# Norm chain of layer 2 ahead of the sort's comparisons, and the sort's first turn one step later

## The chip, the cores and the metric

The kernel runs on one core of one Trainium2 chip, all in float32. The metric is the device time of one execution in microseconds (us); less is better. A core has five engines that work side by side, each through its own queue in order: TensorE (PE, matrix products), VectorE (DVE), ScalarE (ACT), GpSimd (POOL) and SyncE (SP, which here only issues DMA transfers; ACT and POOL issue some too).

## The reference, cut to what matters

The input is one image x of 1024 channels by 64 x 64 pixels. Four layers follow, each of the form `x = x + layer(groupnorm(x))` with 32 groups of 32 channels.

```python
x = x + L0(_gn(x))     # a scan over the channels
x = x + L1(_gn(x))     # einsum('oi,nihw->nohw', weight, x) + bias
x = x + L2(_gn(x))     # state-space layer: projections, convolution, tokens in a permuted order, scan, gate, projection
x = x + L3(_gn(x))     # einsum('oi,nihw->nohw', weight, x) + bias

def _mobius_perm(mobius, H, W):          # in L2: depends on the parameter `mobius` alone
    ...
        perms.append(jnp.argsort(score)) # one permutation of the 4096 tokens for each of two heads
```

Two things matter here. The group norm of layer 2 needs the mean and variance of layer 1's result over all pixels, so it can only be finished when layer 1 is. And the sort (`argsort`) depends on no activation, so its work can be done at any time ahead of layer 2's gather of tokens.

## The kernel before, in words

**Layer 1.** `pointwise` computes the 1024 x 1024 product by `run` and `multiply`: one level of a Strassen-like scheme, seven block products in place of eight. The image is cut into four pairs of 512-pixel columns (order 3, 2, 0, 1), and each pair's outputs into NG = 2 groups. So there are 4 x 2 x 7 = 56 steps, i = 0 to 55. In one step PE does one block product (8 matmuls of 128 x 128 by 128 x 512; the trace records each as two). The seven products of a group come in the order b21, b11, b22, t2, t3, t1, t4, named after the right-hand operand. After a product, DVE takes it out of PSUM: `put` (L963, one scalar_tensor_tensor with the bias) or `add` (L967, one tensor_tensor, and then L152, the batch norm statistics of the finished piece). Two products of a group accumulate on earlier ones: t2 and t1 go into the PSUM banks of b11, and t4 into those of t3. So a matmul that goes on in a bank comes after DVE's reading of it.

**What lies beside the products.** After each product, the body of the loop at L993 runs once. DVE, PE, POOL and ACT are under a manual schedule there: their queues hold the instructions in the order in which the Python code issues them. The body does, in this order:

- `next(sums, None)` (L994): sums of weights for later layers, on POOL (L454 to L457, L468, L481, L492), with their loads and stores on ACT's DMA queue. It yields True (`busy`) in a step in which it put work on POOL.
- `sort_on(not busy, n)` (L995): goes on with the sort. In a step that isn't busy it may issue up to n comparisons, n from a table by i % 14.
- the norm chain of layer 2 for the first four of the eight channel tiles (L996 to L1007), in steps 49 to 54 only.

**The sort** (`sort_work`, a generator) is a bitonic sort of 2 x 4096 keys that lie as 64 lines of 128. A comparison (`compare`, L351 to L360) is eleven small DVE instructions. From its eighth stage on (k > 7) the lines have to be turned: `turn_over` issues two transposes on PE (L370) into a PSUM tile, and a step later ("take") a copy on ACT (L372) into SBUF. Ahead of each turn stands one tensor_scalar on DVE (L399), which the transposes wait for. `sort_on` does at most one turn or take in a step. In layer 1 the first turn is issued in step 26, after product t1, and its copy in step 27.

**The norm chain** (`moments`, `norm_steps`, `rsqrt`), for tiles FIRST, is spread over steps:

| step | product | what is issued |
|---|---|---|
| 49 | b21 | four bn_aggr on DVE (L185, tile gn2a_mv) |
| 50 | b11 | matmul gn2a_pg on PE (L202): means over groups |
| 51 | b22 | three small DVE operations (L205 to L207, gn2a_d) |
| 52 | t2 | matmul gn2a_pv on PE (L211) |
| 53 | t3 | one DVE operation (L219, gn2a_v), then Ln and Exp on ACT (L172, L173) |
| 54 | t1 | four small DVE operations (L175 to L177, L222); two bn_aggr for the other tiles; four ACT operations (L948) that write the first operands of layer 2 |

In steps 49, 51 and 53 the body also issues two, three and two comparisons of the sort, and ahead of the chain's instructions. Steps 50 and 52 are busy for POOL and have none. The transposes of a later turn are issued in step 54.

**Queues around it.** PE's queue after step 50 is: product b11, gn2a_pg, product b22. ACT's queue around step 53 is: Ln, Exp, then the four stores of the last sum of weights (L500, tile s, 448 KB each), and then the first operands of layer 2. SP's queue has the weight loads (L827, into a ring of five buffers) and, behind them, the loads of layer 2 that need the space of these sums (L1232, L479).

```python
            busy = next(sums, None) if i % 14 < 13 else None
            sort_on(not busy, (0, 0, 0, 0, 3, 2, 1, 2, 1, 3, 3, 3, 0, 0)[i % 14])
            if i == last - 6:
                chain = norm_steps("gn2a", *moments("gn2a", FIRST), len(FIRST), finer=True)
            elif last - 6 < i < last - 1:
                next(chain)
```

Of the kernel before, what the change touches and what calls it, by code (L numbers as in the profile page):

```python
# [94 lines left out]
def tile_net(ctx: ExitStack, tc: tile.TileContext, x, par_d, cst_d, w_d, w2_d, dbcw_d, out):  # L95
# [5 lines left out]
    def ps_tp(name):  # L101
        return psum.tile([P, FB], F32, tag="tp", name=name)
# [57 lines left out]
    def finish_of(steps):  # L160

        while True:
            try:
                next(steps)
            except StopIteration as stop:
                return stop.value
# [13 lines left out]
    def moments(name, tiles, some=None, mv=None):  # L180

        if mv is None:
            mv = small.tile([P, 2, CT], F32, tag="gn_mv", name=f"{name}_mv")
        for i in range(len(tiles)) if some is None else some:
            nc.vector.bn_aggr(mv[:, :, i], stats[:, tiles[i]].rearrange("p a b -> p (a b)"))  # L185
        n = len(tiles)
        return mv if some is not None else (mv[:, 0, :n], mv[:, 1, :n])

    def columns(tiles, norm, norms):

        for i, ct in enumerate(tiles):
            norms[ct] = tuple(v[:, i : i + 1] for v in norm)
# [135 lines left out]
    def sort_work():  # L328

        eng, bits = nc.vector, 7
        flip = cst[: HEADS * NT, CST["flip"]]

        def compare(t, new, bit):
            def two(x):
                v = x.rearrange("p (u s l) -> p u s l", s=2, l=2 ** bit)
                return v[:, :, 0], v[:, :, 1]

            rows, _, w = t.shape
            a, b = two(t.rearrange("p c w -> p (c w)"))
            (ka, kb), (ia, ib) = two(t[:, 0]), two(t[:, 1])
            (ka2, kb2), (ia2, ib2) = two(new[:, 0]), two(new[:, 1])
            over = swap[0][:rows, :, : w // 2]
            same = swap[1][:rows, 0, : w // 2]
            step = swap[1][:rows, 1, : w // 2]
            def like(x):
                return x.rearrange("p (u l) -> p u l", l=2 ** bit)
            for i, (x, y) in enumerate(((ka, kb), (ia, ib))):  # L350
                eng.tensor_tensor(like(over[:, i]), x, y, ALU.is_gt)  # L351
            eng.tensor_tensor(like(same), ka, kb, ALU.is_equal)
            eng.tensor_tensor(same, same, over[:, 1], ALU.mult)
            eng.tensor_tensor(ka2, ka, kb, ALU.min)
            eng.tensor_tensor(same, same, over[:, 0], ALU.add)
            eng.tensor_tensor(like(step), ib, ia, ALU.subtract)
            eng.tensor_tensor(kb2, ka, kb, ALU.max)
            eng.tensor_tensor(step, step, same, ALU.mult)
            eng.tensor_tensor(ia2, ia, like(step), ALU.add)
            eng.tensor_tensor(ib2, ib, like(step), ALU.subtract)  # L360

        def negate(v):
            eng.tensor_scalar(v, v, -1.0, None, ALU.mult)

        def turn_over(t, new):
            rows, _, w = t.shape
            yield "turn"
            pt = ps_tp("sort")
            for c in range(2):
                nc.tensor.transpose(pt[:w, c * rows : (c + 1) * rows], t[:, c], ident[:rows, :rows])  # L370
            yield "take"
            nc.scalar.copy(new.rearrange("p c w -> p (c w)"), pt[:w, : 2 * rows])  # L372

        now, other = lines
        negate(now.rearrange("p c (u s l) -> p (c u) s l", s=2, l=2)[:, :, 1])
        for k in range(1, 13):
            if k > bits:
                t, t2 = turned_
                yield from turn_over(now, t)
                for bit in reversed(range(k - bits)):  # L380
                    yield "compare"
                    compare(t, t2, bit)
                    t, t2 = t2, t
                yield from turn_over(t, now)
            for bit in reversed(range(min(k, bits))):
                yield "compare"
                compare(now, other, bit)
                now, other = other, now
            if k + 1 < bits:
                v = now.rearrange("p c (u t s l) -> p (c u) t s l", t=2, s=2, l=2 ** k)  # L390
                negate(v[:, :, 0, 1])
                negate(v[:, :, 1, 0])
            elif k + 1 == bits:
                v = now.rearrange("p c (s l) -> p c s l", s=2)
                for s in range(2):
                    eng.tensor_scalar(v[:, :, s], v[:, :, s], flip[:, s : s + 1], None, ALU.mult)
            elif k < 12:
                i = k - bits + 2
                eng.tensor_scalar(now, now, flip[:, i : i + 1], None, ALU.mult)  # L399
        eng.tensor_copy(order_i, now[:, 1])  # L400
        yield "take"
        nc.gpsimd.dma_start(perm_d.rearrange("(a p) o -> a (p o)", p=P), order_i)
        yield "take"
        for h in range(HEADS):
            r0, full = h * LC + S, (NK - 1) * LT
            perm = perm_d[h * N : (h + 1) * N]
            for idx in (src, dst_):
                nc.gpsimd.dma_start(idx[r0 : r0 + LT, : NK - 1],
                                  perm[:full].rearrange("(k r) o -> r (k o)", r=LT))
                nc.gpsimd.dma_start(idx[r0 : r0 + N - full, NK - 1 :], perm[full:])  # L410
# [3 lines left out]
    def sort_on(quiet, n):  # L414


        while coming[0] is not None:
            was = coming[0]
            if was == "compare":
                if n == 0 or not quiet:  # L420
                    return
                n -= 1
            coming[0] = next(order, None)
            if was != "compare" or coming[0] != "compare":
                return
# [360 lines left out]
    def b_tile(name, k, pair):  # L786
        return bpool.tile([P, FB], F32, tag=name, name=f"{name}_{pair}_{k}")
# [157 lines left out]
    def normed(norm):  # L945
        def make(t, ct, nb):
            scale, bias = norm[ct]
            nc.scalar.activation(t, X[nb][:, ct, :], AF.Identity, bias=bias, scale=scale)  # L948
        return make


    def pointwise(name, m, bias_name, order, src, dst):
        norm = {}
        columns(range(CT), finish_of(norm_steps(f"gn{name}", mean1, var1)), norm)

        def before(pair):
            for nb in (2 * pair, 2 * pair + 1):
                if X[nb] is None:
                    load(nb, src)

        def put(m, o, nb, ps):
            part = X[nb][:, o, :]
            nc.vector.scalar_tensor_tensor(part, ps, pcol(bias_name, o), part, ALU.add, ALU.add)  # L963

        def add(m, o, nb, ps):
            part = X[nb][:, o, :]
            nc.vector.tensor_tensor(part, ps, part, ALU.add)  # L967
            take_stats(nb, o)

        def after(pair):  # L970
            for nb in (2 * pair, 2 * pair + 1):
                save(nb, dst)

        yield from run(order, [m], normed(norm), put, add, before, after, quick=True)
# [17 lines left out]
    with tc.manual_schedule(engines={E_.DVE, E_.PE, E_.Pool, E_.Activation}):  # L992
        for i, _ in enumerate(pointwise("l1", W1, "b1", [3, 2] + EARLY, x0_d, x1_d)):  # L993
            busy = next(sums, None) if i % 14 < 13 else None  # L994
            sort_on(not busy, (0, 0, 0, 0, 3, 2, 1, 2, 1, 3, 3, 3, 0, 0)[i % 14])  # L995
            if i == last - 6:  # L996
                chain = norm_steps("gn2a", *moments("gn2a", FIRST), len(FIRST), finer=True)
            elif last - 6 < i < last - 1:
                next(chain)
            elif i == last - 1:  # L1000
                columns(FIRST, finish_of(chain), norm2)
                mv2 = moments("gn2b", SECOND, range(2))
                name = f"{WX}_{EARLY[0]}"
                begun = {"name": name, **{b: [b_tile(b, k, name) for k in range(2)] for b in ("b21", "b11")}}
                for b, row in (("b21", 1), ("b11", 0)):
                    for k in range(2):
                        normed(norm2)(begun[b][k], row * KH + k, 2 * EARLY[0])  # L1007
        for _ in sums:
            pass
    sum_pool.__exit__(None, None, None)  # L1010
# [34 lines left out]
    with tc.tile_pool(name="l2a", bufs=2) as pa, tc.tile_pool(name="l2a2", bufs=1) as pa2, \  # L1045
# [185 lines left out]
        with tc.manual_schedule(engines={E_.DVE, E_.PE, E_.Pool, E_.Activation}):  # L1231
# [3 lines left out]
            ends, i, chain, quiet = iter(()), -1, None, False  # L1235
# [618 lines left out]
```

## Time and profile before

| what | value |
|---|---|
| time, median of 3 runs | 2684.88 us (2682.02 to 2690.34) |
| the profiled execution: time | 2685.99 us |
| the profiled execution: span of its records | 2684.1 us |
| PE busy | 2564.7 us (96% of the span) |
| DVE busy | 1833.2 us (68%) |
| POOL busy | 1215.3 us (45%) |
| ACT busy | 1079.5 us (40%) |
| mean granted TensorE clock | 0.984 of full speed |
| layer 1's products on PE | from 225 us to 626.7 us |

The span is the time from the first to the last record; some 1.9 us of the execution lie around it. The rest of the document uses these views. The list of waits says which instruction stood at the head of an engine's queue for how long, and whose end released it ("PE a <- DVE b"). A timeline gives start, duration, engine, line, operation, operands and count; in square brackets stands the idle time of the engine just ahead. The table by windows gives for each stretch the busy time of PE, PE's weight loads, DVE, ACT and POOL, with counts, and then the granted TensorE clock (1.00 is full speed), the DMA share and GB/s. A busy time includes time in which an instruction has started and is held inside its engine.

### The profile page before, as it was taken

The numbers are of one execution on the slowest core, as the hardware profiler recorded it, in microseconds if no ns is written. First come the engines' busy times: TensorE is split into PE (matmuls) and PEld (weight loads), VectorE is DVE, ScalarE is ACT, GpSimd is POOL, SyncE is SP. The second block draws the span as 40 slices with busy tenths as digits, with TensorE's granted clock in tenths as the row PEclk, the third lists the DMA queues.
The fourth block names the chain that finished last, engine by engine and source line by source line (L and its number), as shares of the span: only waits on it lengthen the run. The fifth ranks groups of instructions, "written<-read, shape, count | busy, mean of one in ns | idle before, by whom it ended". The sixth has DMA issues, their size and how long they took to land.

```text
span 2684.1 us, 30608 instructions
## 1 busy us (share of the span) xinstructions
PE 2564.7 (96%) x9520; PEld 1712.4 (64%) x9520; DVE 1833.2 (68%) x3870; ACT 1079.5 (40%) x1835; POOL 1215.3 (45%) x1100
## 2 busy tenths in 40 slices
PE   4788999999999999999999999999999999899998
PEld 3674444444555555444454448888888888788887
DVE  7996866655555564367787775677585775877877
ACT  3783110103556564466767663332233223312120
POOL 4154123242132243146474635566575565554544
PEclk9897999999999999999999999999999999999999
DMA  7245467547565577487667946889899798888896
GB/s 291 99 169 204 138 239 251 174 150 241 142 175 142 139 194 179 123 267 238 206 208 237 311 152 199 235 254 293 227 304 259 245 309 220 270 293 297 301 315 213
DMA packets 422741, 597.22 MB, mean 223 GB/s; under 512 B 141972, under 2 KB 210707, under 8 KB 419508
## 3 DMA queue, kind: packets, MB, share of 16 engines
q1 hardware_dynamic: 298020, 367.89, 43.4%
q10 hardware_dynamic: 91456, 136.33, 14.5%
q0 software_dynamic: 33104, 91.04, 13.3%
q8 instruction: 77, 1.26, 0.2%
q14 instruction: 84, 0.69, 0.1%
HBM read 435.10 MB, written 160.05 MB: 222 GB/s over the span
## 4 chain that ended last, share of the span: by engine, by line
PE 80%; DVE 10%; ACT 6%; DMA 2%; issue 1%; POOL 0%; DVEq 0%; ACTq 0%; SPq 0%; POOLq 0%
PE mm L844 36%; PE q_P5P L1728 5%; PE q_P6P L1728 5%; PE q_P7P L1728 5%; PE q_P3P L1728 5%; PE q_P4P L1728 5%; PE q_P2P L1728 5%; PE q_P1P L1728 5%; PE py L1375 2%; PE l2pt L1090 2%; DVE xt L632 1%; DVE cvp L1071 1%; DVE stats L554 1%; ACT b L948 1%; ACT xt L598 1%
## 5 line engine op out<-in xcount | busy, mean ns | idle before, releaser
L844 PE MATMUL mm<-t,w 128*128 128x512 f32 x1536 | 683.9, 596 | 0.0
L844 PE MATMUL mm<-b,w 128*128 128x512 f32 x1152 | 514.4, 598 | 4.0 <-ACT b L948 2.9
L844 PEld LDWEIGHTS mm<-t,w 128*128 128x128 f32 x1536 | 286.9, 191 | 323.1 <-issue 316.3
L844 PEld LDWEIGHTS mm<-b,w 128*128 128x128 f32 x1152 | 216.0, 191 | 252.3 <-issue 241.3
L1384 POOL DMA_INDIRECT y_rows<-g,dst x74 | 73.3, 990 | 184.3 <-ACT g L1380 171.7
L1071 DVE SCALAR_TENSOR_TENSOR cvp<-xs,par,cvp 128x512 f32<-128x512 f32 x128 | 95.3, 753 | 76.8 <-ACT cvp L1068 74.5
L1697 ACT COPY qQ<-q_P5P 128x512 f32<-128x512 f32 x48 | 28.1, 585 | 295.1 <-PE q_P5P L1728 288.8
L468 POOL TENSOR_TENSOR s<-s 128x256 f32<-128x256 f32 (+3 forms) x120 | 129.9, 1088 | 7.5
L1378 ACT COPY g<-py 8x512 f32<-8x512 f32 x146 | 83.8, 574 | 107.5 <-PE py L1375 101.7
L1122 DVE TENSOR_TENSOR xs<-mm,xs 128x512 f32<-128x512 f32 x64 | 41.8, 684 | 116.1 <-PE mm L844 116.1
L1098 POOL TENSOR_TENSOR acc<-l2xt,acc 128x136 f32<-128x136 f32 x56 | 27.8, 497 | 192.4 <-ACT l2xt L1092 191.4
L963 DVE SCALAR_TENSOR_TENSOR image<-mm,par,image 128x512 f32<-128x512 f32 x64 | 47.1, 746 | 96.4 <-PE mm L844 96.4
L1090 PEld LDWEIGHTS l2pt<-both,cv 128*128 128x128 f32 x512 | 76.3, 190 | 36.2 <-issue 22.5
L802 POOL TENSOR_TENSOR t<-t,b 128x512 f32<-128x512 f32 x40 | 55.7, 1419 | 91.8 <-DVE t L802 91.7
L1496 ACT ACTIVATE qb<-x_x_b,gn_bias,gn_r_r 128x512 f32<-128x512 f32 x64 | 48.8, 807 | 113.2 <-DVE qQ L1658 37.3
L948 ACT ACTIVATE b<-image,gnl_bias,gnl_r_r 128x512 f32<-128x512 f32 x48 | 37.2, 808 | 141.6 <-PE mm L844 113.3
L1728 PE MATMUL q_P1P<-t_b,wq_P1P 128*128 128x256 f32 x384 | 92.3, 385 | 1.5 <-POOL t_b L1492 1.5
L1728 PE MATMUL q_P4P<-t_t,wq_P4P 128*128 128x256 f32 x384 | 90.9, 380 | 1.4 <-DVE qV L1705 1.4
L1728 PE MATMUL q_P6P<-t_t,wq_P6P 128*128 128x256 f32 x384 | 90.8, 379 | 0.2 <-DMA wq_P6P<-s_d 0.2
L1728 PE MATMUL q_P5P<-t_t,wq_P5P 128*128 128x256 f32 x384 | 90.8, 379 | 0.0
L1728 PE MATMUL q_P7P<-t_t,wq_P7P 128*128 128x256 f32 x384 | 90.7, 379 | 0.0
L1728 PE MATMUL q_P2P<-t_b,wq_P2P 128*128 128x256 f32 x384 | 90.7, 379 | 0.0
(418 smaller groups left out, 5906.7 us busy)
## 6 DMA issues: line engine op xcount, KB each, us to landing
w<-s_d SPq DMA_DIRECT2D x96, 512.0 KB
w<-in_w_dram SPq DMA_DIRECT2D x72, 512.0 KB
x_x_b<-x_d ACTq DMA_DIRECT2D x28, 1024.0 KB
image<-x_d SPq DMA_DIRECT2D x12, 2048.0 KB
wq_P6P<-s_d SPq DMA_DIRECT2D x84, 256.0 KB
wq_P7P<-s_d SPq DMA_DIRECT2D x84, 256.0 KB
wq_P5P<-s_d SPq DMA_DIRECT2D x84, 256.0 KB
wq_P3P<-s_d SPq DMA_DIRECT2D x84, 256.0 KB
```

Of the source, the lines that this page charges most:

```text
L468: eng.tensor_tensor(out, a, b, ALU.subtract)
L802: eng.tensor_tensor(B[name][k], B[one][k], B[two][k], ALU.subtract)
L844: nc.tensor.matmul(to[o], w[:, k, o * P : (o + 1) * P], B[name][k], start=(fresh and k == 0), stop=(k == KH - 1), skip_group_check=True)
L948: nc.scalar.activation(t, X[nb][:, ct, :], AF.Identity, bias=bias, scale=scale)
L963: nc.vector.scalar_tensor_tensor(part, ps, pcol(bias_name, o), part, ALU.add, ALU.add)
L1071: nc.vector.scalar_tensor_tensor(cv, xo[:, at + t : at + t + FB], pcol("dww", 3 * o + t), cv, ALU.mult, ALU.add)
L1090: nc.tensor.matmul(pt[:, q * NV : (q + 1) * NV], cv[:, (q0 + q) * P : (q0 + q + 1) * P], both[:, o, :], start=True, stop=True)
L1375: nc.tensor.matmul(py, G2[k % 2], rows[k][:, :DH], start=True, stop=True)
L1378: nc.scalar.copy(rows[k + 1][h * LC : h * LC + S, :DH], py[h * LC : h * LC + S])
L1384: nc.gpsimd.indirect_dma_start(out=y_views[k % len(y_views)][:, :], out_offset=bass.IndirectOffsetOnAxis(ap=dst_[:, k : k + 1], axis=0), i ...
L1496: nc.scalar.activation(tile_of(j, name)[:, k], held[j, "x", name][:, k], AF.Identity, bias=bias, scale=scale)
L1728: nc.tensor.matmul(ps[:, o, :], w[:, k, o * P : (o + 1) * P], rhs[:, k, :], start=(new and o == 0 and k == 0), stop=(k == 1), skip_group_c ...
```

## The change

Nothing is added or removed: every engine has the same instructions, and some of them stand elsewhere in its queue.

1. The call of `sort_on` is moved to the end of the loop's body. In steps 49, 51 and 53 the chain's DVE instructions now stand ahead of the comparisons of the same step. In step 54 the chain's last instructions stand ahead of the sort's transposes in the code; they are on other engines.
2. The sort yields once more ("take") ahead of its first turn (k = 8). The two transposes of that turn go from behind product t1 (step 26) to behind product t4 (step 27) in PE's queue, past eight matmuls, and its copy from step 27 to step 28: in ACT's queue it goes from ahead of to behind the two DMA issues that save the finished pair of the image (L141). All later turns and comparisons stand in the steps where they stood.

POOL's and SP's queues hold their instructions in the same order as before.

```diff
@@ sort_work
         for k in range(1, 13):
             if k > bits:
                 t, t2 = turned_
+                if k == bits + 1:
+                    yield "take"
                 yield from turn_over(now, t)
@@ layer 1
         for i, _ in enumerate(pointwise("l1", W1, "b1", [3, 2] + EARLY, x0_d, x1_d)):
             busy = next(sums, None) if i % 14 < 13 else None
-            sort_on(not busy, (0, 0, 0, 0, 3, 2, 1, 2, 1, 3, 3, 3, 0, 0)[i % 14])
             if i == last - 6:
                 chain = norm_steps("gn2a", *moments("gn2a", FIRST), len(FIRST), finer=True)
...
                     for k in range(2):
                         normed(norm2)(begun[b][k], row * KH + k, 2 * EARLY[0])
+            sort_on(not busy, (0, 0, 0, 0, 3, 2, 1, 2, 1, 3, 3, 3, 0, 0)[i % 14])
         for _ in sums:
             pass
```

## The prediction

> **What bounds the kernel now.** I read the page first: which engine the chain that ended last runs on.
>
> ```profile
> PE 80%; DVE 10%; ACT 6%; DMA 2%; issue 1%; POOL 0%; DVEq 0%; ACTq 0%; SPq 0%; POOLq 0%
> ```
>
> PE bounds it, and is busy 96% of the span. So a change to DVE's order is worth only what it takes from PE's waits. Next, the list of PE's waits from 224 to 700 us, which holds layer 1 and the start of layer 2:
>
> ```profile
> PE gn2a_pg L202 <- DVE gn2a_mv L185: 4.0, 1, 4.0
> PE sort L370 <- DVE lines L399: 3.7, 1, 3.7
> PE mm L844 <- ACT b L948: 2.9, 2, 2.4
> PE mm L844 <- ACT xs L1114: 1.1, 1, 1.1
> ```
>
> Two waits concern the change: the first matmul of the norm chain waits 4.0 us for its bn_aggr (step 50), and a turn of the sort waits 3.7 us. PE's timeline places the first:
>
> ```profile
> 574.83 10.89 PE L844 MATMUL mm<-b,w 128*128 128x512 f32 x25
> 589.72 0.36 PE L202 MATMUL gn2a_pg<-gn2a_mv,cst 128*128 128x4 f32 x2 [4.00 <-DVE gn2a_mv L185]
> 589.94 8.81 PE L844 MATMUL mm<-b,w 128*128 128x512 f32 x16
> 598.58 7.03 PE L844 MATMUL mm<-t,w 128*128 128x512 f32 x16
> 605.45 0.28 PE L211 MATMUL gn2a_pv<-gn2a_d,cst 128*128 128x4 f32 x2
> ```
>
> PE ends b11 at 574.83 + 10.89 = 585.72 and stands until 589.72. The product after the wait takes 598.58 - 589.94 = 8.64 us, the next one 605.45 - 598.58 = 6.87: it is slow too. DVE's timeline in that time:
>
> ```profile
> 579.57 2.22 DVE L351 TENSOR_TENSOR swap<-lines 64x64 f32<-64x64 f32 x2
> ...
> 581.96 1.98 DVE L353 TENSOR_TENSOR swap<-swap,swap 64x64 f32<-64x64 f32 x1
> ...
> 584.00 2.09 DVE L355 TENSOR_TENSOR swap<-swap,swap 64x64 f32<-64x64 f32 x1
> ...
> 588.53 1.05 DVE L185 BATCH_NORM_AGGREGATE gn2a_mv<-stats 128x2 f32<-128x48 f32 x4
> 589.50 0.62 DVE L967 TENSOR_TENSOR image<-mm,image 128x512 f32<-128x512 f32 x1
> ```
>
> The two comparisons start at 579.57 and end at 588.53, 8.96 us, where an undisturbed comparison takes 1.72 (581.96 to 588.53 holds such ones: the second starts at 586.81 and ends at 588.53). Three of their instructions last about 2 us in place of 0.21. POOL's timeline has four sums in a row there:
>
> ```profile
> 577.46 2.08 POOL L492 TENSOR_TENSOR s<-s 128x896 f32<-128x896 f32 x1 [6.36 <-DMA s_d<-s]
> 579.62 6.40 POOL L468 TENSOR_TENSOR s<-s 128x896 f32<-128x896 f32 x3
> ```
>
> The step was taken for quiet when the code was issued; POOL runs late, behind a store. Last, the table by windows after the wait; the granted clock is the third figure from the end:
>
> ```profile
> 590.00:592.00 2.00, 2.00 (x5) 0.93 (x5) 1.93 (x4) 0.00 (x0) 0.00 (x0) 0.77 0.00 0
> 592.00:594.00 2.00, 2.00 (x3) 0.67 (x2) 0.17 (x1) 0.00 (x0) 0.00 (x0) 0.50 0.00 0
> 594.00:596.00 2.00, 2.00 (x5) 0.91 (x4) 0.65 (x1) 0.00 (x0) 0.00 (x0) 0.87 0.00 0
> ```
>
> The clock fell to a half for some time after PE had stood.
>
> [...] 2.0 to 2.2 us stalls against POOL operations of 2.1 us. A bn_aggr has one SBUF input [...]; no row shows one under a POOL sum, but bn_stats (L152, one input too) took 0.69 us at 567.6 to 570.3, where POOL's sums ran, as without them. [...] 4.00 us idle, then 0.50.
>
> **The change part by part.**
>
> *Step 49, bn_aggr first.* DVE is free for it at 579.57 (end of the second put, L963). Four bn_aggr take 1.05, so gn2a_mv is there at 580.62. PE asks for it at 585.72: 5.1 us of slack, the wait of 4.00 goes. If POOL did hold each bn_aggr, they would end by 586.02 (end of POOL's sums) + 1.05 = 587.07, and the wait left would be 1.35, under the 4.00. I take zero.
>
> *The slow clock after it.* The windows give 2 x 0.23 + 2 x 0.50 + 2 x 0.13 = 1.72 us lost; the products give 8.64 - 6.87 = 1.77. I take 1.7. It lies between zero and the loss after the other wait of 3.7 us, where 16 matmuls (32 records, 506.89 to 523.54) took 16.65 against 2 x 6.87: 2.9. So 4.0 to 6.9 with the wait, and I take 4.0 + 1.7 = 5.7.
>
> *What is late instead.* The comparisons of step 49 now start at 580.62. At worst none ends before POOL's last sum: 586.02 + 2 x 1.72 = 589.5. Behind them on DVE stand the add operations of step 50 (L967, 0.62 to 0.69 each, L152 between), and PE's product t2 goes on in the bank that the first of them reads: free at 589.5 + 0.65 = 590.2. PE comes to t2 at 598.58 - 5.7 = 592.9. Slack 2.7 us: no new wait. Both adds with statistics end near 592.2; the puts of b22 then run at most 2.6 us after their matmuls, and their banks are next written two products later.
>
> *Step 51, gn2a_d first.* In the kernel before, gn2a_d ended at 605.05 behind three comparisons, and PE issued gn2a_pv at 605.45 without a wait: 0.4 of slack. With PE 5.7 earlier, the old order would now have cost a wait; in the new one it follows the put at 598.78 + 0.67 - 5.7 = 593.8, and ends at 594.3 against PE's 599.75. So this edit is worth nothing against before, but it keeps the 5.7. The three comparisons (5.15 us) push the put of t2 back to 599.5; its bank is next needed by t1 at 606.9.
>
> *Step 53, gn2a_v first.* Ln and Exp move from 617.40 to about 608 (609.31 to 612.74 are puts; the second ends at 613.4 - 5.7 = 607.7). What uses them, L175, stands on DVE behind step 54's adds, at 623.58 before, so nothing comes of it but the general 5.7. Behind Exp on ACT stand four stores of 448 KB (L500), issued 617.72 to 621.35 before: they now go at about 608, some 10 us earlier, and SP's L1232, which waited for them, follows earlier. PE waited for no DMA in this stretch, so this gains nothing on PE. Its cost is the second rival below.
>
> *Step 54.* The chain's end is on DVE and ACT, the transposes on PE; both keep their queues. Zero.
>
> *The first turn a step later.* DVE and PE at that turn, from the two timelines:
>
> ```profile
> 411.92 0.34 DVE L399 TENSOR_SCALAR lines<-lines,cst 64x256 f32<-64x256 f32 x1
> ...
> 394.62 18.19 PE L844 MATMUL mm<-t,w 128*128 128x512 f32 x42
> 412.75 0.34 PE L370 MATMUL sort<-cst,lines 64*128 64x64 f32 x2
> ```
>
> L399 ends at 412.26, PE comes at 412.75 with no idle time: slack 0.5, so nothing is removed in this execution. Moved, the transposes cost PE the same 0.3 us seven us later. The copy on ACT (0.24, at 414.29 before) now stands behind the two saves of the image, whose issue waited until 422.57 for DVE, so it runs at about 423.6; the next comparison, which reads it, ran at 455.19. Cover 31 us: zero. Behind it on ACT are stores (L500), 0.24 later: zero. The turn that did wait, 3.7 us at 506.51, is a later one and isn't moved.
>
> *After layer 1.* PE, DVE and ACT begin layer 2 as one chain (the chain of waits runs from gn2a_pg through PE's products to the first operands), so all of it shifts by 5.7. PE's later waits come from DVE, ACT or POOL work that follows PE's own, and its waits for DMA are 0.5 us in all. I take the 5.7 as kept.
>
> Against the profiled execution: 2685.99 - 5.7 = 2680.3. Its time is 1.1 above the median of 2684.88. From the median: 2684.88 - 5.7 = **2679.2 us**, -0.21%. Measurement of this kernel can tell about 0.3% (8.05 us) from no change, so the forecast is "within 0.3%", on the faster side.
>
> **The rivals.**
> *A, the forecast*: 2679.2. Chance 0.66.
> *B, part of the wait stays*: bn_aggr held by POOL, wait 1.35, no slow clock: 5.7 - 1.35 = 4.35, so 2680.5. [...] Down to 2.7 (2682.2) if the clock still falls. 0.13.
> *C, more than seen*: in runs without the profiler the first turn may also wait, with a slack of only 0.5 us; its twin at 506.51 cost 3.7 and 2.9 of slow clock. Then 5.7 + 6.6 = 12.3: 2672.6. Against: the profile shows no wait, and POOL is idle there until 417.48. 0.12.
> *D, the wait only moves*: comparisons of step 49 ending after 592.2 (2.7 beyond my worst) hold the adds and so t2. At 596, say, t2 waits 596 + 0.65 - 592.9 = 3.75, and the gain is 1.95: 2682.9. 0.06.
> *E, slower*: the stores, now early, crowd out the weights of layer 2's first products. Stores 1.8 MB, two weight loads 1.05 MB and the saves of the image 4.2 MB are 7.1 MB; the weights for layer 2's t2 are needed at 642.97 - 5.7 = 637.3. If all of it stood ahead of them from 608 on, at the mean 171 GB/s of 560 to 700 us, they would land at 649.5: a wait of 12.2 and 1.7 of slow clock, less 5.7: +8.2, 2693. It turns to a loss below 7.1 MB / 35 us = 203 GB/s. Against: the trace has 257 to 395 GB/s where DMA is busy (633 to 650 us), and the weights are issued ahead of the saves. 0.03.
>
> **How the numbers follow.** Runs before lie between -2.9 and +5.5 us about their median, so I give a measured A 3 to 4 us either way: 2675.5 to 2683. B and D lie inside or at the edge. I leave out C, E and A's tails, about 0.18: range 2674 to 2685. Faster by over 0.3% is under 2676.8: nearly all of C (0.11) and a sixth of A and B by spread (0.11): 0.22. Slower: E, 0.03. The rest 0.75.
>
> **What would show it.** In the profile after: no wait of gn2a_pg for gn2a_mv; bn_aggr at about 579.6 with 1.05 us for four (1.0 to 7 would be B); clock 1.00 through 586 to 600; gn2a_pv near 599.7 and layer 2's first product near 621, from 626.73; t2 without a wait at 592.9 (a wait for L967 is D); no wait for w after 621 (E); the first turn's transposes near 420. The prediction fails if layer 2's start moves but the end doesn't.

## The result and the profile after

| | before | changed |
|---|---|---|
| median of 12 runs | 2684.63 us (2682.02 to 2690.34) | 2676.97 us (2674.79 to 2680.99) |
| profiled execution, span | 2684.1 us | 2677.1 us |

The ratio of the times is 0.9972, with a 95% interval of 0.9963 to 0.9980: 5.4 to 9.9 us less. The forecast was 5.7 less (2679.2 us, range 2674 to 2685) and "within 0.3%"; the change came out at 0.28%.

First the list of PE's waits from 224 to 700 us in the changed kernel, whole. Lines below L379 keep their numbers, later ones have gone up by 2 (L399 is L401, L844 is L846, L967 is L969):

```profile
PE sort L370 <- DVE lines L401: 3.9, 1, 3.9
PE mm L846 <- ACT b L950: 2.9, 2, 2.4
PE mm L846 <- ACT xs L1116: 1.1, 1, 1.1
```

The wait of gn2a_pg for gn2a_mv is gone, the other three stand as they were. PE's timeline around it:

```profile
572.27 13.90 PE L846 MATMUL mm<-b,w 128*128 128x512 f32 x32
586.00 0.28 PE L202 MATMUL gn2a_pg<-gn2a_mv,cst 128*128 128x4 f32 x2
586.14 7.11 PE L846 MATMUL mm<-b,w 128*128 128x512 f32 x16
593.09 7.03 PE L846 MATMUL mm<-t,w 128*128 128x512 f32 x16
599.96 0.28 PE L211 MATMUL gn2a_pv<-gn2a_d,cst 128*128 128x4 f32 x2
```

No idle time stands in brackets. Product b22 takes 593.09 - 586.14 = 6.95 us, where it took 8.64. The table by windows says the same of the clock (third figure from the end):

```profile
590.00:592.00 2.00, 2.00 (x6) 0.95 (x5) 1.97 (x4) 0.00 (x0) 0.00 (x0) 1.00 0.00 0
592.00:594.00 2.00, 2.00 (x6) 0.81 (x5) 0.73 (x3) 0.00 (x0) 0.00 (x0) 1.00 0.00 0
594.00:596.00 2.00, 2.00 (x6) 0.91 (x5) 1.86 (x14) 0.00 (x0) 0.00 (x0) 1.00 0.56 205
```

DVE's timeline shows what runs in place of the old order:

```profile
580.00 1.05 DVE L185 BATCH_NORM_AGGREGATE gn2a_mv<-stats 128x2 f32<-128x48 f32 x4
580.97 0.81 DVE L351 TENSOR_TENSOR swap<-lines 64x64 f32<-64x64 f32 x2
581.71 2.09 DVE L352 TENSOR_TENSOR swap<-lines 64x64 f32<-64x64 f32 x1
583.83 2.12 DVE L353 TENSOR_TENSOR swap<-swap,swap 64x64 f32<-64x64 f32 x1
...
588.52 0.21 DVE L360 TENSOR_TENSOR lines<-lines,swap 64x64 f32<-64x64 f32 x1
588.65 0.68 DVE L969 TENSOR_TENSOR image<-mm,image 128x512 f32<-128x512 f32 x1
```

and POOL's timeline what ran beside it:

```profile
577.34 2.07 POOL L494 TENSOR_TENSOR s<-s 128x896 f32<-128x896 f32 x1 [6.16 <-DMA s_d<-s]
579.49 6.38 POOL L470 TENSOR_TENSOR s<-s 128x896 f32<-128x896 f32 x3
```

POOL's sums stand where they stood. The four bn_aggr run through under them in 1.05 us, as they did without POOL; the comparisons behind them are still held, about 2.1 us at a time, and end at 588.73, hardly later than before (588.60, where L185 could start). Nobody on PE's path waits for them any more.

How much of the gain lies in this place: I follow the same two instructions of ACT through both traces, first in the kernel before, then in the changed one:

```profile
565.16 0.36 ACT L372 COPY lines<-sort 64x256 f32<-64x256 f32 x1 [47.47 <-DMA s<-in_w_dram]
648.37 1.33 ACT L1123 ACTIVATE xs<-xs,par 128x512 f32<-128x512 f32 x2 [3.68 <-DVE xs L1122]
```

```profile
565.60 0.37 ACT L372 COPY lines<-sort 64x256 f32<-64x256 f32 x1 [47.47 <-DMA s<-in_w_dram]
642.89 1.33 ACT L1125 ACTIVATE xs<-xs,par 128x512 f32<-128x512 f32 x2 [3.68 <-DVE xs L1124]
```

The copy near 565 us, ahead of step 49, starts 0.44 us later than before; the first activation of layer 2's xs starts 5.48 us earlier. So the stretch between is 5.92 us shorter. The spans differ by 7.0; the other 1.1 us come in small steps far from the change (the 0.44 lost ahead of it, then 0.33 gained between 900 and 1100 us, 0.42 between 2100 and 2200, 0.77 after 2550). Whether those belong to the change is the first question of the experiments.

### The profile page after: what moved, and what is told of

Same layout as the page of the kernel before. It is cut to its first block, busy times and chain, and to the rows that moved or that the text cites. A ratio compares the mean times of both kernels' runs of the same rounds, so it can differ in the third digit from the quotient of the medians.

```text
span 2677.1 us, 30610 instructions
## 1 busy us (share of the span) xinstructions
PE 2563.8 (96%) x9520; PEld 1714.8 (64%) x9520; DVE 1838.1 (69%) x3870; ACT 1079.2 (40%) x1835; POOL 1214.9 (45%) x1100
## 4 chain that ended last, share of the span: by engine, by line
PE 81%; DVE 9%; ACT 6%; DMA 2%; issue 1%; POOL 0%; DVEq 0%; ACTq 0%; SPq 0%; POOLq 0%
PE mm L846 36%; PE q_P6P L1730 5%; PE q_P5P L1730 5%; PE q_P7P L1730 5%; PE q_P2P L1730 5%; PE q_P4P L1730 5%; PE q_P3P L1730 5%; PE q_P1P L1730 5%; PE py L1377 2%; PE l2pt L1092 2%; DVE xt L634 2%; DVE cvp L1073 1%; DVE stats L556 1%; ACT b L950 1%; ACT xt L600 1%
## 5 line engine op out<-in xcount | busy, mean ns | idle before, releaser
L846 PE MATMUL mm<-t,w 128*128 128x512 f32 x1536 | 683.4, 596 | 0.0
L846 PE MATMUL mm<-b,w 128*128 128x512 f32 x1152 | 512.6, 596 | 4.0 <-ACT b L950 2.9
L846 PEld LDWEIGHTS mm<-t,w 128*128 128x128 f32 x1536 | 287.3, 191 | 323.1 <-issue 315.6
L846 PEld LDWEIGHTS mm<-b,w 128*128 128x128 f32 x1152 | 215.5, 191 | 250.4 <-issue 238.5
L1707 DVE TENSOR_TENSOR qV<-q_P4P,qV 128x512 f32<-128x512 f32 x96 | 64.9, 686 | 38.7 <-PE q_P4P L1730 37.0
```

The costliest lines, as they stand in the source:

```text
L846: nc.tensor.matmul(to[o], w[:, k, o * P : (o + 1) * P], B[name][k], start=(fresh and k == 0), stop=(k == KH - 1), skip_group_check=True)
L1707: nc.vector.tensor_tensor(to, ps, to, ALU.add)
```

## The experiments

My theory: the wait of gn2a_pg and the slow clock after it are the whole gain; POOL's hold on the comparisons makes the wait; steps 51 to 54 and the later first turn bring nothing. The rivals: the later first turn gives the 1.8 us by which the measured 7.7 exceeds the traced 5.9; step 51's order is needed to keep the gain; the slow clock has another cause.

All kernels are the kernel before with an edit, but for the last, which starts from the changed one. In the summary, "stretch" is the shift of L1123 less that of the copy near 565 us, from the traces as above (times not rounded first, so the last digit can differ by one from the rounded lines). For e7 a second stretch, from ACT's work near 317 us to that copy, is given in its section.

| kernel | ratio to before | 95% interval | stretch, us | wait of gn2a_pg, us |
|---|---|---|---|---|
| changed kernel | 0.9972 | 0.9963 to 0.9980 | -5.92 | none |
| e1: chain ahead, old first turn | 0.9976 | 0.9969 to 0.9983 | -5.93 | none |
| e2: later first turn alone | 1.0001 | 0.9993 to 1.0010 | -0.01 | 4.0 |
| e3: bn_aggr alone ahead | 0.9977 | 0.9968 to 0.9986 | -5.93 | none |
| e4: all of the chain but bn_aggr ahead | 0.9997 | 0.9988 to 1.0005 | 0.01 | 4.0 |
| e5: old order, POOL's last sums left out | 0.9979 | 0.9971 to 0.9988 | -5.93 | none |
| e6: bn_aggr between the two comparisons | 0.9987 | 0.9981 to 0.9994 | -3.64 | 2.0 |
| e7: changed kernel, next turn later too | 0.9951 | 0.9938 to 0.9965 | -5.93 | none |

### e1 and e2: the two parts of the change

e1 has the call of `sort_on` at the end of the body, as in the change; e2 has only this:

```diff
                 t, t2 = turned_
+                if k == bits + 1:
+                    yield "take"
                 yield from turn_over(now, t)
```

> The kernel before, with the call of sort_on at the end of the loop's body and no later first turn. Theory (all of the gain is the wait of gn2a_pg and the slow clock after it): as the changed kernel's trace, 5.9 us less than before, no wait for gn2a_mv, granted clock 1.00 from 586 to 600 us. Rival (the later first turn gives the part of the measured 7.7 us that the trace doesn't show): as much as the changed kernel less 1.8, so the two experiments e1 and e2 add up, 5.9 and 1.8.

> The kernel before, with the first turn of the sort a step later and the old place of sort_on. Theory: no difference (0 us, within 1), the wait of 4.0 us for gn2a_mv and a stretch of half clock after it stay. Rival (the first turn waits in executions without the profiler): 1.8 us less, up to 6.6.

e1: 0.9976, that is 4.6 to 8.3 us less, and the stretch is 5.93 shorter. e2: 1.0001, from 1.9 us less to 2.7 more. The two of PE's waits in e2 that concern the change (the others are as before):

```profile
PE gn2a_pg L202 <- DVE gn2a_mv L185: 4.0, 1, 4.0
PE sort L370 <- DVE lines L401: 3.8, 1, 3.8
```

The chain's place is the gain. The later first turn shows none; its rival of 1.8 us lies at the edge of e2's interval, that of 6.6 outside it. In the changed kernel's trace the transposes stand at 420.12, where the forecast had them near 420, and PE waits for them neither there nor at the old place.

### e3 and e4: which step of the chain

```diff
+            if i == last - 6:
+                chain = norm_steps("gn2a", *moments("gn2a", FIRST), len(FIRST), finer=True)
             sort_on(not busy, (0, 0, 0, 0, 3, 2, 1, 2, 1, 3, 3, 3, 0, 0)[i % 14])
-            if i == last - 6:
-                chain = norm_steps("gn2a", *moments("gn2a", FIRST), len(FIRST), finer=True)
-            elif last - 6 < i < last - 1:
+            if last - 6 < i < last - 1:
```

is e3; e4 is the complement: these two lines at the end of the body, behind `sort_on`, and all the rest of the chain ahead of it.

> The kernel before, with only step 49's four bn_aggr ahead of that step's comparisons; in the steps after it the comparisons stay ahead of the chain, and the first turn is the old one. Theory: DVE's work in step 51 starts from a put that waits for PE, so it comes earlier with PE; gn2a_d keeps its slack of 0.4 us, gn2a_pv doesn't wait: 5.9 us less than before. Rival (the prediction's own sentence that step 51's old order would now cost a wait): gn2a_d stays near 605.05 while PE comes at 599.8, a wait of up to 5.3 us, so 0.6 us less than before and the slow clock with it. The four stores behind Exp on ACT go out near 611.5 in place of 608; if the time is that of the changed kernel, their earlier issue is worth nothing.

> The kernel before, with the chain ahead of the comparisons in steps 50 to 54, but in step 49 the bn_aggr behind them as before; old first turn. Theory: 0 us (within 1), wait of 4.0 us for gn2a_mv and half clock after it. Rival (the chain's later steps or the earlier stores bring part of it): 1 to 2 us less than before.

e3 has the whole gain, e4 none. In e3, DVE's gn2a_d still stands behind three comparisons in step 51, and PE doesn't wait for it. DVE's timeline of e3, and then PE's:

```profile
600.05 0.16 DVE L207 TENSOR_TENSOR gn2a_d<-gn2a_d,gn2a_mv 128x4 f32<-128x4 f32 x1
```

```profile
593.66 7.03 PE L844 MATMUL mm<-t,w 128*128 128x512 f32 x16
600.52 0.28 PE L211 MATMUL gn2a_pv<-gn2a_d,cst 128*128 128x4 f32 x2
```

gn2a_d ends at 600.21, PE asks at 600.52: 0.3 of slack, about what it was before (0.4). The record's sentence on step 51 falls. In e4 the same operation ends at 600.06, five us ahead of PE at 605.52, and it is worth nothing. The stores behind Exp go out at 612.80 in e3 and at 608.42 in the changed kernel; the stretch is the same to 0.01 us, so their time doesn't matter either.

### e5: is it POOL?

```diff
+            if m != WG or c != 3:
                 eng.tensor_tensor(a22, a21, a22, ALU.add)
...
```

with all four sums under the condition.

> The kernel before in its old order, without the last four sums of weights on POOL (577.46 to 586.02 us); this leaves those sums out, so the gate's products are computed from unsummed weights. Theory [...]: the two comparisons take 2 x 1.72 us, gn2a_mv is there at 579.6 + 3.45 + 1.05 = 584.1, ahead of PE at 585.7: no wait, clock 1.00, 5.9 us less than before. Rival (the comparisons are slow by themselves there, or DVE is late for another reason): the wait of 4.0 us stays, 0 us.

DVE's timeline of e5, the two comparisons' first lines and bn_aggr:

```profile
580.03 0.34 DVE L351 TENSOR_TENSOR swap<-lines 64x64 f32<-64x64 f32 x2
...
581.74 0.34 DVE L351 TENSOR_TENSOR swap<-lines 64x64 f32<-64x64 f32 x2
...
583.46 1.05 DVE L185 BATCH_NORM_AGGREGATE gn2a_mv<-stats 128x2 f32<-128x48 f32 x4
```

Two comparisons take 583.46 - 580.03 = 3.43 us, gn2a_mv is there at 584.51, and PE comes at 586.02 without a wait. So in the old order the wait was made by POOL's sums: without them the old order is as good as the new one. The stretch is 5.93 shorter, and the kernel's ratio 0.9979.

### e6: a shorter wait

Does the clock fall after any wait, or only after a long one? In the kernel before it stood at 0.50 with waits of 3.74 and 4.00 us. The theory here is that a wait of some 2 us costs no more than itself; it was a supposition of the author's, and no trace had shown it.

```diff
-            sort_on(not busy, (0, 0, 0, 0, 3, 2, 1, 2, 1, 3, 3, 3, 0, 0)[i % 14])
+            n = (0, 0, 0, 0, 3, 2, 1, 2, 1, 3, 3, 3, 0, 0)[i % 14]
+            sort_on(not busy, 1 if i == last - 6 else n)
             if i == last - 6:
                 chain = norm_steps("gn2a", *moments("gn2a", FIRST), len(FIRST), finer=True)
+                sort_on(not busy, 1)
```

> The kernel before, with step 49's bn_aggr between its two comparisons, all else in the old order. The first comparison ends near 586.8 as before, so gn2a_mv is there at 587.9 and PE waits 2.2 us in place of 4.0. Theory [...]: clock stays 1.00, loss 2.2, so 3.7 us less than before. Rival (the clock falls after any such wait): 2.0 us less than before. Rival 2 (the slow stretch isn't tied to the wait): the product after it takes 8.6 us again.

PE's timeline of e6 and then its table by windows:

```profile
587.24 0.36 PE L202 MATMUL gn2a_pg<-gn2a_mv,cst 128*128 128x4 f32 x2 [2.04 <-DVE gn2a_mv L185]
587.46 7.11 PE L844 MATMUL mm<-b,w 128*128 128x512 f32 x16
594.41 7.03 PE L844 MATMUL mm<-t,w 128*128 128x512 f32 x16
```

```profile
590.00:592.00 2.00, 2.00 (x6) 0.93 (x5) 1.97 (x4) 0.00 (x0) 0.00 (x0) 1.00 0.00 0
592.00:594.00 2.00, 2.00 (x6) 0.80 (x6) 0.04 (x1) 0.00 (x0) 0.00 (x0) 1.00 0.00 0
```

PE waits 2.04 us, the clock stays at 1.00, and b22 takes 6.95. Halving the wait gives 3.64 of 5.92 us: the slow clock goes with the second half. Where it sets in, these runs don't fix: one wait of 2.04 us stands without it here, seven of 3.6 to 4.0 with it (last section), and from 2342.1 to 2348.9 us of the kernel before the clock was at 0.50 where PE had been idle for 1.36 us ahead of 2339.67 and for 2.52 ahead of 2342.86.

### e7: the other wait of the same kind

The wait that stands first in the changed kernel's list has the same shape: comparisons under POOL's sums, then L401, then transposes on PE. PE's timeline of the changed kernel there:

```profile
507.18 0.44 PE L370 MATMUL sort<-cst,lines 64*128 64x64 f32 x2 [3.91 <-DVE lines L401]
507.55 16.59 PE L846 MATMUL mm<-t,w 128*128 128x512 f32 x32
```

The three comparisons start at 497.11 (L358 to L360 of the first take 1.3 us each beside POOL's sums), and L401 behind them at 506.69; undisturbed, three take 3 x 1.72 = 5.2 us, so L401 would be done near 502.7, ahead of PE at 503.27. This working is from the trace; POOL's sums were not left out here. The first turn of k = 9 can be given a step more too:

```diff
-                if k == bits + 1:
+                if k in (bits + 1, bits + 2):
                     yield "take"
```

> The changed kernel, with the sort's next turn of the lines (step 39, the first turn of k = 9, for which PE waits 3.9 us on L401 and then runs 16 matmuls in 16.4 us in place of 13.7) a step later too. Theory (same cause as the wait removed: comparisons held by POOL, then a slow clock): both go, 3.9 + 2.7 = 6.6 us less than the changed kernel, 14 less than before. Rival (the wait moves to the next reader, PE's next product or the later copy): no more than 1 us less than the changed kernel.

The median is 2670.25 us, 6.7 under the changed kernel's 2676.97 and 0.9951 of the kernel before. PE's timeline of e7 at that turn, and its list of waits from 226 to 645 us, whole:

```profile
487.83 20.76 PE L846 MATMUL mm<-t,w 128*128 128x512 f32 x48
508.52 0.34 PE L370 MATMUL sort<-cst,lines 64*128 64x64 f32 x2
508.79 7.13 PE L846 MATMUL mm<-t,w 128*128 128x512 f32 x16
```

```profile
PE mm L846 <- ACT xs L1116: 1.1, 1, 1.1
PE mm L846 <- ACT b L950: 0.5, 1, 0.5
```

PE comes to the transposes at 508.52, L401 ended at 505.35, and the next product takes 6.97 us. From 317 us to the copy near 565 the trace is 6.74 shorter than before (the changed kernel: 0.06), near the theory's 6.6. But this isn't a fixed price: in e2 and e6, which keep the wait, the same stretch is 1.3 and 1.5 us shorter than before, since the slow clock after the wait was shorter there (last section); against those two, e7 gains about 5.3. All five runs of e7 (2669.09 to 2671.54) lie below all twelve of the changed kernel, but the two were not timed side by side: against the kernel before, timed beside each, the ratios 0.9951 and 0.9972 make 5.6 us between them.

## Why the prediction was right, point by point

- *The wait of step 49 goes.* Right: bn_aggr from 580.00, 1.05 us for four, PE at 586.00 without a wait. That POOL could hold the bn_aggr (rival B) is refuted: they ran from 580.00 to 581.05 while POOL summed from 579.49 to 585.87.
- *The slow clock goes.* Right; in e6, with a wait of 2.04 us in place of 4.00, it didn't come either. 8.64 - 6.95 = 1.69 us, forecast 1.7. That the size fits so well is in part luck: in e2 the same wait of 4.00 us cost 8.42 - 6.95 = 1.47, and the turn's wait cost up to 2.9 (last section).
- *The sum.* Forecast 5.7, the stretch shows 5.92. The 0.2 that the forecast lacks: without a wait PE takes gn2a_pg 0.17 ahead of the modelled end of the product before it (572.27 + 13.90 - 586.00), and the matmul after it starts 0.14 later in place of 0.22. 4.00 + 0.17 + 0.08 + 1.69 = 5.94.
- *What is late instead.* Right: the comparisons ended at 588.73 (worst case given: 589.5), the first add at 589.33, and t2 started at 593.09 without a wait. Rival D didn't come.
- *Step 51.* Wrong. The record said that with PE 5.7 us earlier "the old order would now have cost a wait", and that the edit "keeps the 5.7". It left DVE's end of gn2a_d at its old clock time. But the three comparisons ahead of it start from a put that waits for PE, so they come earlier with PE; e3 keeps the whole gain. The edit is worth nothing in either sense. This step had no term in the sum, so the total didn't suffer.
- *Steps 53 and 54, the stores.* Right: Ln at 608.10 (about 608), stores 9.3 us earlier, no effect on the stretch (e3), no wait for a DMA (rival E).
- *The first turn.* Right: e2 is 1.0001. Rival C, up to 6.6 us, is outside its interval. The copy ran at 425.96 (forecast about 423.6), behind the saves, which were issued from 424.92; the next comparison that reads it came at 455.69, so the delay cost nothing.
- *Kept to the end.* Right as far as it can be told. The shift of 5.48 to 5.5 us at the start of layer 2 stood to 900 us, and after that small steps came on top. e4, whose stretch shows no gain, has such steps too: 1.7 us less than before between 900 and 1100 us, 1.4 more between 2200 and 2400, 1.5 less after 2550. So steps of this size come without the change, and the 7.7 us of the first comparison (5.4 to 9.9) agree with 5.9. The other kernels with the same stretch, e1, e3 and e5, came out at 6.4, 6.2 and 5.6 us less by their ratios. What makes these steps was not tried. That the measured change stayed "within 0.3%" has some luck in it: the interval, 0.20 to 0.37%, reaches over that line.

## What to carry to other kernels

Where one engine's work holds up some of another's instructions, as POOL's sums did with the comparisons here (2.1 us in place of 0.21), the price of an instruction is set by what stands in front of it in its own queue: put the few instructions for which the bounding engine waits ahead of those that can be held, even if the total work is the same. Count for such a wait not only its idle time but the slow clock behind it, which here was 1.7 us on 4.0; and find whether the work behind it starts from the clock or from the engine that has been moved, before pricing it. One wait removed is a reason to look for its twin: the same cause stood 83 us earlier in the same list, and was worth about 6 us more (5.6 by the ratios, 6.7 by the medians and the trace).

## What the runs showed of the hardware

- Four bn_aggr of 128 x 48 in float32 took 1.05 us under a running POOL operation on SBUF and 1.05 without one; comparisons of two SBUF operands beside the same sums took up to 2.1 us an instruction in place of 0.21.
- Beside sums that followed each other on POOL, DVE got one or two instructions through per sum: in the changed kernel L351, L352 and L353 end at 581.8, 583.8 and 586.0, once per sum; in the kernel before, one short instruction ran between two held ones.
- The slow clock came with the turn's waits of 3.74 us in the kernel before, 3.91 in the changed kernel, 3.8 in e2 and 3.6 in e6, and with the wait of 4.00 us of gn2a_pg in the kernel before, e2 and e4; it did not come after that of 2.04 us in e6. It lasted 3.41 or 6.83 us, and did not start with PE's restart: in the kernel before it set in at 591.09, 1.4 us after PE had gone on, and at 505.76, while PE still waited. Its table by windows over these two stretches:

```profile
505.77:512.58 6.81, 6.07 (x9) 2.81 (x10) 1.88 (x5) 0.00 (x0) 0.00 (x0) 0.50 0.01 3
591.10:594.49 3.39, 3.39 (x5) 1.35 (x4) 1.03 (x2) 0.00 (x0) 0.00 (x0) 0.50 0.00 0
```

- So waits of about the same length cost different amounts of clock. After 4.00 us of idle time the next product took 8.64 us in the kernel before and in e4, and 8.42 in e2, in place of 6.95. After the turn's wait, 16 matmuls lost 2.9 us (before) and 2.7 (changed kernel), where the slow clock lasted 6.83 us, but 1.6 (e2) and 1.7 (e6), where it lasted 3.41. What decides which of the two lengths comes was not tried.
